# Cross-attention and feed-forward: a fixed TensorE order for the last group of heads, output products one step behind the scores, loads spread over more steps, other PSUM banks for the second pair

## Chip, cores and metric

The kernel runs on one core of one Trainium2 chip. The metric is device time in microseconds (us) for one execution; lower is better. A profile of one execution gives the times of single instructions.

The engines of the core are TensorE (PE, matrix products; the loading of its weights is listed as PEld), VectorE (DVE), ScalarE (ACT), GpSimd (POOL) and SyncE (SP, which here issues nearly all DMAs). Each engine carries out its own list of instructions in a fixed order, and waits in it for semaphores of the others.

## What is computed

One block of cross-attention and a gated feed-forward layer, in float32, on eight batches of 128 tokens of width 512, with 32 heads of width 128. Cut to what matters:

```python
x = x + attention(layernorm(x), ctx, mask, position_bias, ln_weight, w_q, w_k, w_v, w_out)
x = x + ffn(layernorm(x), Wg, Wu, Wd, ag, au, ad)

def attention(h, ctx, m, bias, ...):
    q = heads(rmsnorm(h) * ln_weight @ w_q.T)          # b, 128, 32, 128
    k, v = heads(ctx @ w_k.T), heads(ctx @ w_v.T)
    score = softmax(where(m, einsum('bqhd,bkhd->bhqk', q, k) + bias, -inf))
    attn = einsum('bhqk,bkhd->bqhd', where(m, score, 0), v)
    return h + attn.reshape(b, 128, 32 * 128) @ w_out.T

def ffn(x, ...):
    gate, up = (x @ Wg.T) * ag, (x @ Wu.T) * au        # 1376 wide
    return ((silu(gate) * up) @ Wd.T) * ad
```

## The kernel before

**Groups of heads.** The 32 heads are worked on in eight groups of four (`NG` = 8, `GH` = 4). All queries are projected first (`mm_q`) and stored in HBM as `queries`. Then the loop at line 492 runs over the groups `g`, and inside it line 511 runs over the eight batches `b`. The key and value projections (`mm_k`, `mm_v`) of group g+1 are a Python generator, `products`. It is advanced by three or four product groups per batch (line 520), so that they lie between the attention matmuls of group g.

**Seven products for eight.** Each large product is cut into 2 x 2 blocks and formed from seven block products instead of eight. The sums of blocks that this needs are formed by `sums_a` and `sums_b`: `S_k` and `S_v` of the projection weights on POOL, `T_o` of the output weights on POOL, and `S_a` of the attended values on DVE.

**One batch of attention.** `probabilities` (line 293) adds bias and mask on POOL (L297), forms the scores `sc` on PE (L302), adds the two on DVE, takes the maximum, exponentiates on ACT and divides on DVE. `transpose_p` (line 332) turns the probabilities in 32 x 32 blocks on DVE (`tt`), writes them to HBM (`turned`, L337) and reads them back as `pT` with four DMAs (L342). `attend` (line 354) multiplies by the values (`av`, L358), copies the result out of PSUM on ACT (`aT`) and stores it in HBM as `att`. The variable `pend` keeps three batches between scores and `attend`: scores of batch b are followed by `av` of batch b-3.

**Output products.** `out_products` (line 463) runs over the groups for one pair of batches. For each group `attended` (line 451) loads `a` from `att` (L453) and forms its sums `S_a` (L194 to L197). Then 14 matmuls (28 in the trace's count) go into four PSUM banks `m` (L470). The first pair's output products are interleaved with the last group of heads (line 526), the other three pairs follow after the loop. Each pair is followed by its residual and its second normalization; the transposes of the result (`tp`, L153) stand behind the third output product of the next pair.

**Weights.** `load_wo(g)` loads the output weights of group g, 1 MB, and forms their sums on POOL. The first two are loaded in groups 1 and 2 of the loop. At the start of the last group the pools of the projections are closed (line 503), and in their room a pool `wosB` for five more groups is opened; the eighth group's weights lie in four tiles of the pool `acts`.

**What sets the order.** The program is a list that a scheduler sorts for each engine: an instruction may be placed in front of earlier ones when its operands are expected sooner. Within one engine the resulting order is then fixed. Tiles of a pool wait until the tile before in the same place is released. The lines that set the order in question:

```python
        if g == NG - 1:
            proj.close()
            wos = pools(outp)("wosB", NG - 3, reuse_waits="tile")
...
            advance(3)
            for _ in range(4 if b % 2 else 3):
                next(products, None)
            if g == NG - 1:
                if b < NG - 3:
                    load_wo(b + 2)
                if b < NG - 1:
                    next(first_out)
```

Of the kernel before, what the change touches and what calls it, by code (L numbers as in the profile page):

```python
# [20 lines left out]
MASKED = 3.0e38  # L21
FLOOR = -1.0e38
TINY = 1.0e-30


@with_exitstack
def xattn_ffn_kernel(
# [49 lines left out]
    proj, rows, attn = ExitStack(), ExitStack(), ExitStack()  # L77
    toks = pools(proj)("toks", reuse_waits="tile")
    spool = pools(proj)("spool", 2, reuse_waits="tile")
    wpool = pools(proj)("wpool", 3, reuse_waits="tile")  # L80
    hpool = pools(rows)("hpool", side="right", reuse_waits="tile")
    ps_mm, ps_tp, ps = (pools(attn)(f"ps{n}", 2, space=PSUM) for n in ("mm", "tp", "at"))

    def load_w(name, src):
        t = wpool.tile([P, DC, GW], F32, tag="w", name=name)
# [65 lines left out]
    def transposed(y, tp):  # L151
        for c in range(DC):
            nc.tensor.transpose(tp[:, c, :], y[:, bass.ts(c, P)], ident)  # L153
        return tp
# [138 lines left out]
    def probabilities(g, b, qT, kT, pb):  # L293
        cols = bass.ts(b, S)
        n = f"{g}_{b}"
        s = work.tile([P, GH, S], F32, tag="s", name=f"s_{n}", bufs=3)
        nc.gpsimd.tensor_tensor(  # L297
            s, pb, mneg[:, b : b + 1, :].to_broadcast([P, GH, S]), ALU.add
        )
        sc = ps.tile([P, GH, S], F32, tag="sc", name=f"sc_{n}")  # L300
        for j in range(GH):
            nc.tensor.matmul(  # L302
                sc[:, j, :], qT[:, j, bass.ts(b % 2, S)], kT[j][:, cols], start=True, stop=True
            )
# [49 lines left out]
    def attend(g, b, pT, v):  # L354
        n = f"{g}_{b}"
        av = ps.tile([P, GH, S], F32, tag="av", name=f"av_{n}")
        for j in range(GH):
            nc.tensor.matmul(  # L358
                av[:, j, :], v[b // 2][:, b % 2, bass.ts(j, P)], pT[:, :, j, :],
                start=True, stop=True,  # L360
            )
        aT = work.tile([P, GH, S], F32, tag="aT", name=f"aT_{n}")
        nc.scalar.copy(aT, av)  # L363
        nc.sync.dma_start(att[g][b // 2][:, b % 2], aT)

    pend = []

    def advance(lag):
# [62 lines left out]
    def load_wo(g):  # L431
        src = woT[bass.ts(g, GW), :].rearrange("(c p) n -> p c n", p=P)
        if g == NG - 1:
            up, dn, t12, t4 = (
                acts.tile([P, 2, D], F32, tag="a", name=f"wo{g}_{k}") for k in range(4)
            )
            nc.sync.dma_start(up, src[:, :HC])
            nc.sync.dma_start(dn, src[:, HC:])
            t1, t2, t4 = (
                t.rearrange("p (c n) -> p c n", c=HC) for t in (t12[:, 0], t12[:, 1], t4[:, 0])  # L440
            )
        else:
            w = wos.tile([P, GH, D], F32, tag="w", name=f"wo{g}")
            nc.sync.dma_start(w, src)
            t = wos.tile([P, 3, HC, HW], F32, tag="T", name=f"T_o{g}")
# [17 lines left out]
    def out_products(i, order, banks):  # L463

        m = by_product(banks)
        for g in order:
            sa = attended(g, i)
            for k, n in enumerate((1, 2, 6, 7, 4, 5, 3)):
                for c in range(HC):
                    nc.tensor.matmul(  # L470
                        m[n], sa[n][:, c, :], wo_t[g][n][:, c, :],
                        start=(g == order[0] and c == 0 and k % 2 == 0),
                        stop=(g == order[-1] and c == HC - 1), skip_group_check=True,
                    )
            yield


    def load_bias(g):
# [13 lines left out]
    for g in range(NG):  # L492
        kT, v = kvs.pop(g)
        pb = biases.pop(g)
        if g + 1 < NG:
            biases[g + 1] = load_bias(g + 1)
        if g + 2 < NG:
            kv_w[g + 2] = load_kv(g + 2)
        products = kv(g + 1, kvs) if g + 1 < NG else iter(())
        if g in (1, 2):  # L500
            load_wo(g - 1)
        if g == NG - 1:
            proj.close()
            wos = pools(outp)("wosB", NG - 3, reuse_waits="tile")

            first_banks = [
                pl.tile([P, 2, HW], F32, tag=tag, name=f"m{k}_0")
                for k, (pl, tag) in enumerate(((ps_mm, "mm"), (ps_mm, "mm"), (ps_tp, "pt"), (ps_tp, "pt")))
            ]
            first_out = out_products(0, list(range(NG)), first_banks)  # L510
        for b in range(B):
            if b % 2 == 0:
                qT = ahead.pop((g, b // 2))
                at = todo.index((g, b // 2)) + 2
                if at < len(todo):
                    ahead[todo[at]] = load_queries(*todo[at])
            p = probabilities(g, b, qT, kT, pb)
            pend.append((g, b, transpose_p(g, b, p), v))
            advance(3)
            for _ in range(4 if b % 2 else 3):  # L520
                next(products, None)
# [12 lines left out]
    mv2 = const.tile([P, B, 2], F32, name="mv2")  # L534
    rs2 = const.tile([P, B], F32, name="rs2")

# [36 lines left out]
    def norm2_T(b, y):  # L573
        th, cols = b * S // 512, bass.ds(b * S % 512, S)
        if (0, th) not in h2:
            for f in range(2):
                h2[f, th] = acts.tile([P, HC, 512], F32, tag="a", name=f"h2_{f}_{th}")
        tp = transposed(y, ps.tile([P, DC, P], F32, tag="tp", name="tp2", bufs=1))
        nc.vector.tensor_copy(h2[0, th][:, :, cols], tp[:, :HC])
        nc.scalar.copy(h2[1, th][:, :, cols], tp[:, HC:])  # L580

    x1, ys, banks = [], [], first_banks
    for i in range(B // 2):
        last = i + 1 == B // 2
        order = [2, 3, 4, 5, 6, 7, 0, 1] if last else list(range(NG))
        if i:
            banks = [ps.tile([P, 2, HW], F32, tag="m", name=f"m{k}_{i}") for k in range(4)]
            for n, _ in enumerate(out_products(i, order, banks)):
                if n == 2:
                    for y in ys:  # L590
                        norm2_T(*y)
        m = by_product(banks)
        x1.append(acts.tile([P, 2, D], F32, tag="a", name=f"x1_{i}"))
        for k in range(2):
            b = 2 * i + k
            nc.sync.dma_start(x1[i][:, k, :], x[b])
            nc.scalar.activation(
                x1[i][:, k, :], x1[i][:, k, :], AF.Identity,
                bias=res_bias[:, b : b + 1], scale=res_scale[:, b : b + 1],
            )  # L600
        if last:
            outp.close()
        else:
            residual(i, x1[i], m, banks)
            ys = norm2(i, x1[i])
# [165 lines left out]
```

## Time and profile before

| What | us |
|---|---|
| median of three runs | 1152.23 (1151.07 to 1153.02) |
| profiled execution | 1152.01 |
| its span, first to last instruction | 1150.2 |
| PE busy | 1120.0 (97% of the span) |
| DVE, ACT, POOL busy | 502.3, 318.1, 297.9 |
| output matmuls `m` (L470): mean of one | 0.392 (`wo`,`a` form) |
| scores `sc` and `av`: mean of one | 0.277 |
| POOL bias sum and sums of weights, 128 x 512 | 1.27 |
| `a` from `att`, 512 KB: issue to landing, median | 3.5 |
| `turned`, 256 KB, and `pT`, 64 KB: the same | 2.1 and 2.4 |

Matmuls are pipelined, so the time from one start to the next is shorter than the duration of one: four `m` matmuls that are listed with 1.03 us follow one another every 0.86 us. A wait in brackets in a timeline is idle time of the engine just before the instruction, with what ended it. The page's slices are 28.8 us each.

### The profile page before, as it was taken

How to read it: one execution, taken by the hardware profiler on the slowest of the kernel's cores; microseconds unless marked ns; L12 is line 12 of the kernel's file. 1: busy time of each engine (PE TensorE's matmuls, PEld its weight loads, DVE VectorE, ACT ScalarE, POOL GpSimd, SP SyncE). 2: the span in 40 equal slices, each digit the busy share in tenths (PEclk: the TensorE clock that was granted, in tenths of full speed). 3: DMA queues.
4: the chain of work that ended last, by engine and by line, in shares of the span. 5: the costliest groups of instructions: out<-in, count | busy, mean ns of one | idle time of the engine just before them, and what ended most of it. 6: DMA issues, size and time to landing. Idle time of an engine off the chain costs nothing.

```text
span 1150.2 us, 12321 instructions
## 1 busy us (share of the span) xinstructions
PE 1120.0 (97%) x4286; PEld 731.4 (64%) x4286; DVE 502.3 (44%) x957; ACT 318.1 (28%) x899; POOL 297.9 (26%) x255
## 2 busy tenths in 40 slices
PE   6999999999999999999999999789999999999998
PEld 3564444445867777686958689678888864444445
DVE  4541111116555555555555557824433242434311
ACT  2521112223444344444344443301000022223000
POOL 5331221116333333333223315620000034220000
PEclk9999999999999999999999999899999999999999
DMA  9114432257555455555554347865232332110000
GB/s 284 41 37 149 175 114 110 110 197 259 175 166 175 151 186 174 168 182 183 179 173 152 129 139 218 275 192 171 78 104 65 109 128 73 36 37 1 18 29 28
DMA packets 117533, 154.38 MB, mean 134 GB/s; under 512 B 12032, under 2 KB 71680, under 8 KB 117472
## 3 DMA queue, kind: packets, MB, share of 16 engines
q1 hardware_dynamic: 114784, 149.93, 40.3%
q10 hardware_dynamic: 2192, 2.10, 0.6%
q0 software_dynamic: 496, 1.58, 0.4%
q8 instruction: 34, 0.56, 0.2%
q14 instruction: 27, 0.22, 0.1%
HBM read 101.14 MB, written 52.43 MB: 134 GB/s over the span
## 4 chain that ended last, share of the span: by engine, by line
PE 91%; DVE 4%; DMA 2%; ACT 1%; issue 1%; POOL 0%; SPq 0%; ACTq 0%; DVEq 0%
PE mm_q L262 17%; PE mm_v L280 16%; PE m L470 16%; PE mm_k L262 16%; PE mm_f L690 9%; PE dn L721 7%; PE sc L302 4%; PE av L358 4%; DMA wk<-in_wkT_dram 1%; DMA wo<-in_woT_dram 1%; PE tp L153 1%; PE up L655 1%; PE gp L655 1%; DVE sg L641 1%; ACT s L312 0%
## 5 line engine op out<-in xcount | busy, mean ns | idle before, releaser
L297 POOL TENSOR_TENSOR s<-pb,mneg 128x512 f32<-128x512 f32 x64 | 81.2, 1269 | 291.1 <-DVE tt L335 217.3
L262 PE MATMUL mm_k<-ctx_sb,wk 128*128 128x512 f32 x256 | 117.8, 604 | 7.2 <-DMA wk<-in_wkT_dram 4.4
L280 PE MATMUL mm_v<-wv,ctx_sb 128*128 128x256 f32 x512 | 115.9, 379 | 0.8 <-DMA wv<-in_wvT_dram 0.8
L262 PE MATMUL mm_q<-hT,wq 128*128 128x512 f32 x256 | 112.5, 592 | 0.0
L312 ACT ACTIVATE s<-s,nmx 128x128 f32<-128x128 f32 x256 | 99.5, 390 | 36.0 <-DVE nmx L309 36.0
L470 PE MATMUL m<-wo,a 128*128 128x256 f32 x400 | 101.5, 392 | 6.6 <-DMA a<-att 6.5
L280 PEld LDWEIGHTS mm_v<-wv,ctx_sb 128*128 128x128 f32 x512 | 95.1, 190 | 14.4 <-DMA wv<-in_wvT_dram 1.6
L363 ACT COPY aT<-av 128x512 f32<-128x512 f32 x64 | 37.5, 586 | 203.3 <-PE av L358 105.4
L262 PE MATMUL mm_k<-ctx_sb,S_k 128*128 128x512 f32 x192 | 88.3, 607 | 4.3 <-DVE k L241 3.9
L470 PEld LDWEIGHTS m<-wo,a 128*128 128x128 f32 x400 | 77.7, 197 | 18.0 <-DMA a<-att 6.8
L262 PEld LDWEIGHTS mm_q<-hT,wq 128*128 128x128 f32 x256 | 48.6, 190 | 60.8 <-issue 60.7
L280 PE MATMUL mm_v<-S_v,ctx_sb 128*128 128x256 f32 x384 | 86.6, 381 | 0.0
L262 PEld LDWEIGHTS mm_k<-ctx_sb,wk 128*128 128x128 f32 x256 | 47.2, 194 | 60.1 <-issue 45.5
L262 PE MATMUL mm_q<-hT,S_q 128*128 128x512 f32 x192 | 85.0, 592 | 0.0
L305 DVE TENSOR_TENSOR s<-sc,s 128x512 f32<-128x512 f32 x64 | 44.2, 690 | 86.8 <-PE sc L302 83.6
L280 PEld LDWEIGHTS mm_v<-S_v,ctx_sb 128*128 128x128 f32 x384 | 71.5, 190 | 11.0 <-DVE v L252 1.8
L302 PEld LDWEIGHTS sc<-k,q 128*128 128x128 f32 x512 | 67.3, 194 | 17.4 <-issue 13.4
L721 PE MATMUL dn<-wd,act 128*128 128x512 f32 (+3 forms) x198 | 75.8, 545 | 0.0
L252 DVE TENSOR_TENSOR q<-q,mm_q 128x512 f32<-128x512 f32 x32 | 22.0, 688 | 114.8 <-PE mm_q L262 114.8
L302 PE MATMUL sc<-k,q 128*128 128x128 f32 x512 | 68.1, 277 | 2.0 <-DMA q<-queries 1.9
L358 PE MATMUL av<-pT,v 128*128 128x128 f32 x512 | 68.1, 277 | 0.0
L262 PEld LDWEIGHTS mm_k<-ctx_sb,S_k 128*128 128x128 f32 x192 | 35.4, 192 | 49.3 <-issue 35.7
(156 smaller groups left out, 1492.1 us busy)
## 6 DMA issues: line engine op xcount, KB each, us to landing
queries<-q SPq DMA_DIRECT2D x32, 512.0 KB, 3.8
q<-queries SPq DMA_DIRECT2D x32, 512.0 KB, 4.4
turned<-tt SPq DMA_DIRECT2D x64, 256.0 KB, 2.1
pT<-turned SPq DMA_DIRECT2D x256, 64.0 KB, 2.4
att<-aT SPq DMA_DIRECT2D x64, 256.0 KB, 2.3
a<-att SPq DMA_DIRECT2D x32, 512.0 KB, 3.5
wq<-in_wqT_dram SPq DMA_DIRECT2D x8, 1024.0 KB, 5.5
wk<-in_wkT_dram SPq DMA_DIRECT2D x7, 1024.0 KB, 6.1
```

The lines of the kernel that those rows point to most:

```text
L262: nc.tensor.matmul(out, w[i][:, c, bass.ts(t, P)], src[i][:, c, :], start=(first and c == 0), stop=(c == HC - 1), skip_group_check=True,)
L280: nc.tensor.matmul(out[:, bass.ts(k, HW)], src[i][:, c, bass.ts(2 * t + k, S)], w[i][:, c, :], start=(first and k == 0 and c == 0), stop=( ...
L297: nc.gpsimd.tensor_tensor(s, pb, mneg[:, b : b + 1, :].to_broadcast([P, GH, S]), ALU.add)
L302: nc.tensor.matmul(sc[:, j, :], qT[:, j, bass.ts(b % 2, S)], kT[j][:, cols], start=True, stop=True)
L305: nc.vector.tensor_tensor(s, sc, s, ALU.add)
L312: nc.scalar.activation(s[:, j, :], s[:, j, :], AF.Exp, bias=nmx[:, j : j + 1], accum_out=sm[:, j : j + 1],)
L358: nc.tensor.matmul(av[:, j, :], v[b // 2][:, b % 2, bass.ts(j, P)], pT[:, :, j, :], start=True, stop=True,)
L363: nc.scalar.copy(aT, av)
L470: nc.tensor.matmul(m[n], sa[n][:, c, :], wo_t[g][n][:, c, :], start=(g == order[0] and c == 0 and k % 2 == 0), stop=(g == order[-1] and c ...
L655: nc.tensor.matmul(o[-1][:m], w[:, c, :m], h2[c // HC, th][:, c % HC, :], start=(c == 0), stop=(c == DC - 1),)
L690: nc.tensor.matmul(out, ws[t][n][:, c, :], h2_t[n][:, c, :], start=(first and c == 0), stop=(c == HC - 1), skip_group_check=True,)
L721: nc.tensor.matmul(o, act[ic][:m, bass.ts(b, S)], wd[:m, ic, cols], start=(n == 0), stop=(n == NI - 1),)
```

## The change

Nearly all edits are on the last group of heads and what follows it.

1. In the last group, every PE instruction (scores, `av`, output products) is recorded through `InOrder`, which keeps the order of the program instead of letting the scheduler sort.
2. The first pair's output products begin at batch 1 instead of batch 0, so that product b-1 follows the scores of batch b. Product 7 comes after `av` of batch 5, and before those of batches 6 and 7. `out_products` asks for the attended values of the next group before it forms the products of the present one.
3. In the group before the last, three fewer product groups of the projections are formed; these three follow the first scores of the last group.
4. The pools `spool` (three buffers instead of two) and `wpool` outlive the projections. Output weights 2, 3 and 4 lie in them, loaded as their tiles come free; 2 is asked for in the group before the last. `wosB` has two buffers instead of five. Weights 3 to 6 are asked for at batches 0 to 3 of the last group and weight 7 at batch 5.
5. The pool of the score and `av` banks is opened first, so that the banks of the first pair's products are others than those the second pair then takes; the pool behind them is split in four and three banks, taken in turn (`Turns`).
6. The two transposes of a pair are placed behind the third and the fourth output product of the next pair, instead of both behind the third.

```diff
+class Turns:
+    def __init__(self, *pools):
+        self.pools, self.n = pools, 0
+    def tile(self, *args, **kw):
+        self.n += 1
+        return self.pools[(self.n - 1) % 7 // 4].tile(*args, **kw)
+class InOrder:
...
+            return self.tc.keep_in_program_order(getattr(self.engine, op)(*args, **kw))
...
-    spool = pools(proj)("spool", 2, reuse_waits="tile")
-    wpool = pools(proj)("wpool", 3, reuse_waits="tile")
+    spool = pools(wts)("spool", 3, reuse_waits="tile")
+    wpool = pools(wts)("wpool", 3, reuse_waits="tile")
-    ps_mm, ps_tp, ps = (pools(attn)(f"ps{n}", 2, space=PSUM) for n in ("mm", "tp", "at"))
+    ps, ps_mm, ps_tp = (pools(attn)(f"ps{n}", 2, space=PSUM) for n in ("at", "mm", "tp"))
...
-            w = wos.tile([P, GH, D], F32, tag="w", name=f"wo{g}")
+            held = g in (2, 3, 4)
+            w = (wpool if held else wos).tile([P, GH, D], F32, tag="w", name=f"wo{g}")
...
-        for g in order:
-            sa = attended(g, i)
+        coming = attended(order[0], i)
+        for n, g in enumerate(order):
+            sa = coming
+            if n + 1 < NG and ahead:
+                coming = attended(order[n + 1], i)
...
-        products = kv(g + 1, kvs) if g + 1 < NG else iter(())
+        if g + 1 < NG:
+            products = kv(g + 1, kvs)
...
+        if g == NG - 2:
+            load_wo(2)
         if g == NG - 1:
-            proj.close()
-            wos = pools(outp)("wosB", NG - 3, reuse_waits="tile")
...
-            first_out = out_products(0, list(range(NG)), first_banks)
+            tensor = InOrder(tc, nc.tensor)
...
-            for _ in range(4 if b % 2 else 3):
+            for _ in range(4 if b % 2 and (g < NG - 2 or b == 3) else 3):
                 next(products, None)
             if g == NG - 1:
-                if b < NG - 3:
-                    load_wo(b + 2)
-                if b < NG - 1:
+                if b == 0:
+                    proj.close()
+                    wos = pools(outp)("wosB", 2, reuse_waits="tile")
...
+                    first_out = out_products(0, list(range(NG)), first_banks)
+                if b < NG - 4 or b == 5:
+                    load_wo(b + 3 if b < NG - 4 else NG - 1)
+                if b:
                     next(first_out)
-    load_wo(NG - 1)
+    advance(2)
+    next(first_out)
     advance(0)
-    next(first_out)
+    tensor = nc.tensor
...
-    ps = pool("psO", 7, space=PSUM, reuse_waits="tile")
+    ps = Turns(
+        pool("psA", 4, space=PSUM, reuse_waits="tile"),
+        pool("psB", 3, space=PSUM, reuse_waits="tile"),
+    )
...
-                if n == 2:
-                    for y in ys:
-                        norm2_T(*y)
+            if n in (2, 3):
+                norm2_T(*ys[n - 2])
```

More of the change, by code (lines that the diff above doesn't have):

```diff
@@ L23, with __init__, __getattr__, call @@
 TINY = 1.0e-30
+class Turns:
[5 more added lines that the diff above has]
+class InOrder:
+    def __init__(self, tc, engine):
+        self.tc, self.engine = tc, engine
+    def __getattr__(self, op):
+        def call(*args, **kw):
+            return self.tc.keep_in_program_order(getattr(self.engine, op)(*args, **kw))
+        return call
 @with_exitstack
@@ L75, in xattn_ffn_kernel @@
     small = pool("small", 4, side="right", reuse_waits="tile")
-    proj, rows, attn = ExitStack(), ExitStack(), ExitStack()
+    proj, rows, attn, wts = ExitStack(), ExitStack(), ExitStack(), ExitStack()
+    spool = pools(wts)("spool", 3, reuse_waits="tile")
+    wpool = pools(wts)("wpool", 3, reuse_waits="tile")
     toks = pools(proj)("toks", reuse_waits="tile")
-    spool = pools(proj)("spool", 2, reuse_waits="tile")
-    wpool = pools(proj)("wpool", 3, reuse_waits="tile")
     hpool = pools(rows)("hpool", side="right", reuse_waits="tile")
-    ps_mm, ps_tp, ps = (pools(attn)(f"ps{n}", 2, space=PSUM) for n in ("mm", "tp", "at"))
+    ps, ps_mm, ps_tp = (pools(attn)(f"ps{n}", 2, space=PSUM) for n in ("at", "mm", "tp"))
     def load_w(name, src):
@@ L301, in probabilities @@
         for j in range(GH):
-            nc.tensor.matmul(
+            tensor.matmul(
                 sc[:, j, :], qT[:, j, bass.ts(b % 2, S)], kT[j][:, cols], start=True, stop=True
@@ L357, in attend @@
         for j in range(GH):
-            nc.tensor.matmul(
+            tensor.matmul(
                 av[:, j, :], v[b // 2][:, b % 2, bass.ts(j, P)], pT[:, :, j, :],
@@ L442, in load_wo @@
         else:
-            w = wos.tile([P, GH, D], F32, tag="w", name=f"wo{g}")
+            held = g in (2, 3, 4)
+            w = (wpool if held else wos).tile([P, GH, D], F32, tag="w", name=f"wo{g}")
             nc.sync.dma_start(w, src)
-            t = wos.tile([P, 3, HC, HW], F32, tag="T", name=f"T_o{g}")
+            t = (spool if held else wos).tile(
+                [P, 3, HC, HW], F32, tag="S" if held else "T", name=f"T_o{g}"
+            )
             up, dn, t1, t2, t4 = w[:, :HC], w[:, HC:], t[:, 0], t[:, 1], t[:, 2]
@@ L461, in by_product, with out_products @@
         return {n: banks[k // 2][:, k % 2, :] for k, n in enumerate((1, 2, 6, 7, 4, 5, 3))}
-    def out_products(i, order, banks):
+    def out_products(i, order, banks, ahead=True):
         m = by_product(banks)
-        for g in order:
-            sa = attended(g, i)
+        coming = attended(order[0], i)
[3 more added lines that the diff above has]
+                coming = attended(order[n + 1], i)
             for k, n in enumerate((1, 2, 6, 7, 4, 5, 3)):
                 for c in range(HC):
-                    nc.tensor.matmul(
+                    tensor.matmul(
                         m[n], sa[n][:, c, :], wo_t[g][n][:, c, :],
@@ L475, in out_products @@
             yield
+            if n + 1 < NG and not ahead:
+                coming = attended(order[n + 1], i)
     def load_bias(g):
@@ L498, in xattn_ffn_kernel @@
             kv_w[g + 2] = load_kv(g + 2)
-        products = kv(g + 1, kvs) if g + 1 < NG else iter(())
+        if g + 1 < NG:
+            products = kv(g + 1, kvs)
         if g in (1, 2):
             load_wo(g - 1)
+        if g == NG - 2:
+            load_wo(2)
         if g == NG - 1:
-            proj.close()
-            wos = pools(outp)("wosB", NG - 3, reuse_waits="tile")
[L506 to L509, printed above, removed]
-            first_out = out_products(0, list(range(NG)), first_banks)
+            tensor = InOrder(tc, nc.tensor)
         for b in range(B):
@@ L519, in xattn_ffn_kernel @@
             advance(3)
-            for _ in range(4 if b % 2 else 3):
+            for _ in range(4 if b % 2 and (g < NG - 2 or b == 3) else 3):
                 next(products, None)
             if g == NG - 1:
-                if b < NG - 3:
-                    load_wo(b + 2)
-                if b < NG - 1:
+                if b == 0:
+                    proj.close()
+                    wos = pools(outp)("wosB", 2, reuse_waits="tile")
+                    first_banks = [
+                        pl.tile([P, 2, HW], F32, tag=tag, name=f"m{k}_0")
+                        for k, (pl, tag) in enumerate(2 * [(ps_mm, "mm")] + 2 * [(ps_tp, "pt")])
+                    ]
+                    first_out = out_products(0, list(range(NG)), first_banks)
+                if b < NG - 4 or b == 5:
+                    load_wo(b + 3 if b < NG - 4 else NG - 1)
+                if b:
                     next(first_out)
-    load_wo(NG - 1)
+    advance(2)
+    next(first_out)
     advance(0)
-    next(first_out)
+    tensor = nc.tensor
     attn.close()
-    ps = pool("psO", 7, space=PSUM, reuse_waits="tile")
+    ps = Turns(
+        pool("psA", 4, space=PSUM, reuse_waits="tile"),
+        pool("psB", 3, space=PSUM, reuse_waits="tile"),
+    )
     mv2 = const.tile([P, B, 2], F32, name="mv2")
@@ L577, in norm2_T, with first_residual @@
                 h2[f, th] = acts.tile([P, HC, 512], F32, tag="a", name=f"h2_{f}_{th}")
-        tp = transposed(y, ps.tile([P, DC, P], F32, tag="tp", name="tp2", bufs=1))
+        tp = transposed(y, ps.pools[1].tile([P, DC, P], F32, tag="tp", name="tp2", bufs=1))
         nc.vector.tensor_copy(h2[0, th][:, :, cols], tp[:, :HC])
         nc.scalar.copy(h2[1, th][:, :, cols], tp[:, HC:])
[L582 to L588, printed above, removed]
-                if n == 2:
-                    for y in ys:
-                        norm2_T(*y)
-        m = by_product(banks)
+    x1 = []
+    def first_residual(i):
         x1.append(acts.tile([P, 2, D], F32, tag="a", name=f"x1_{i}"))
@@ L600, in xattn_ffn_kernel @@
             )
+    first_residual(0)
+    residual(0, x1[0], by_product(first_banks), first_banks)
+    ys = norm2(0, x1[0])
+    for i in range(1, B // 2):
+        last = i + 1 == B // 2
+        order = [2, 3, 4, 5, 6, 7, 0, 1] if last else list(range(NG))
+        banks = [ps.tile([P, 2, HW], F32, tag="m", name=f"m{k}_{i}") for k in range(4)]
+        for n, _ in enumerate(out_products(i, order, banks)):
+            if n in (2, 3):
+                norm2_T(*ys[n - 2])
+        m = by_product(banks)
+        first_residual(i)
         if last:
             outp.close()
+            wts.close()
         else:
```

## The prediction

> **What bounds the kernel now.** I began with the page's chain that ended last and its first list, to see which engine sets the end.
>
> ```profile
> PE   6999999999999999999999999789999999999998
> ...
> PE 91%; DVE 4%; DMA 2%; ACT 1%; issue 1%; POOL 0%; SPq 0%; ACTq 0%; DVEq 0%
> ```
>
> TensorE (PE) is busy in every slice except about the 26th, and 91% of the chain is PE. Elsewhere only less PE work would help, and this change leaves the matmuls as they are. So what matters is time in which PE waits or runs slowly. A table of stages prices it (columns: stretch in us; busy us and instructions of PE, PEld, DVE, ACT, POOL; clock; DMA share; GB/s).
>
> ```profile
> 690.00:720.00 30.00, 29.89 (x184) 27.00 (x182) 21.03 (x42) 9.77 (x38) 14.62 (x12) 1.00 0.71 216
> 720.00:775.00 55.00, 44.28 (x212) 38.22 (x212) 30.69 (x54) 12.43 (x48) 25.46 (x19) 0.90 0.73 233
> 775.00:860.00 85.00, 83.63 (x382) 73.05 (x383) 37.84 (x102) 6.85 (x13) 3.94 (x4) 0.97 0.35 116
> 860.00:935.00 75.00, 74.08 (x346) 64.65 (x345) 21.32 (x56) 4.69 (x9) 11.18 (x16) 1.00 0.38 125
> ```
>
> From 720 to 775, PE is idle for 10.7 of 55 us and its clock falls to 0.90. That is the last group of heads. PE's timeline says for whom it waits (start, length, what, and in brackets the wait before it).
>
> ```profile
> 700.49 1.89 PE L470 MATMUL m<-wo,a 128*128 128x256 f32 x8
> ...
> 717.94 1.95 PE L302 MATMUL sc<-k,q 128*128 128x128 f32 x16
> 721.76 1.13 PE L302 MATMUL sc<-k,q 128*128 128x128 f32 x8 [1.87 <-DMA q<-queries]
> ...
> 729.36 3.51 PE L470 MATMUL m<-wo,a 128*128 128x256 f32 x8 [2.80 <-DMA a<-att]
> 735.55 1.12 PE L470 MATMUL m<-T_o,S_a 128*128 128x256 f32 x4 [2.67 <-DVE S_a L195]
> ...
> 749.84 1.05 PE L358 MATMUL av<-pT,v 128*128 128x128 f32 x8
> 750.73 1.89 PE L470 MATMUL m<-wo,a 128*128 128x256 f32 x8
> ...
> 775.45 3.78 PE L470 MATMUL m<-wo,a 128*128 128x256 f32 x8 [3.65 <-DMA a<-att]
> ...
> 803.91 0.66 PE L153 MATMUL tp<-ident,y 128*128 128x128 f32 x4 [0.92 <-ACT h L580]
> ```
>
> Eight output matmuls take 3.51 us at 729.36, after a wait, and 1.89 us at 750.73. A wait is therefore paid twice: once as idle time and once as slow matmuls behind it. At 717.94 the scores of three batches run one after another with nothing between them.
>
> SyncE's (SP) timeline shows why `a` is late at 729: it was issued behind a 1 MB `wo`, and both behind the round trips of the probabilities.
>
> ```profile
> 705.62 0.34 SPq L337 DMA_DIRECT2D turned<-tt  x1
> ...
> 707.83 1.74 SPq L342 DMA_DIRECT2D pT<-turned  x4
> ...
> 714.70 0.34 SPq L337 DMA_DIRECT2D turned<-tt  x1
> ...
> 719.94 0.43 SPq L444 DMA_DIRECT2D wo<-in_woT_dram  x1
> ...
> 722.45 0.43 SPq L453 DMA_DIRECT2D a<-att  x1
> ...
> 754.70 0.43 SPq L453 DMA_DIRECT2D a<-att  x1
> ```
>
> The loss, with batch rows of this timeline: from the scores at 698.71 to the first pair's last product at 784.26 PE has to do 8 scores and 11 `av` of 0.89 us each (start to start, 698.71 to 699.60) and 8 output products of 6.05 us (700.49 to 706.54), 16.9 + 48.4 = 65.3 us. It takes 85.55. **20.2 us are lost**: 11.0 in the four waits in brackets (1.87, 2.80, 2.67, 3.65), the rest at a slow clock.
>
> [...] 3.51 us for eight matmuls against 1.73 (750.73 to 752.46)[...] after waits of 2.80 us already. [...] here `pT` is issued 2.21 us after its `turned` (705.62 to 707.83). [...] an `S_a` sum takes 0.41 us alone and 1.49 us at 741.85 in DVE's timeline, while POOL forms `T_o`. [...] PE shows no wait at 784.26, where the second pair begins, so the trace has nothing to gain there.
>
> **The change, part by part.** *Fixed order.* By the built program, the last group's PE order becomes: scores b, `av` b-3, output product b-1, for each b; then `av`5, product 7, `av`6, `av`7, second pair. One step is 2 x 0.89 + 6.05 = 7.83 us. The run of scores is gone and the 65.3 us of work stay. Nothing can now overtake a late operand: whatever is late stops PE. So I price each product by when its `a` arrives.
>
> *Three value products kept back.* Three stretches of eight `mm_v` matmuls, 5.18 us together (three such stand between two steps in the chain of waits), move from before the last group's first scores to behind them. Cost nil; they cover the first step. Group 6's steps shrink to 6.96 us. Three of them, 20.9 us, must hold scores to `pT`: 6.9 to the issue of `turned` (698.71 to 705.62) + 2.2 + 1.74 for four `pT` + about 2.4 landing = 13.3. Hidden; uncovered it would cost some 1 us a step.
>
> *Weights earlier.* `wo`2, 3, 4 go to the pools of the projection weights, and 2 and 3 are now loaded before the last group begins. Of the chain's 7.50 us DMA and about 5 us POOL around 720 to 733 nothing remains before product 2. POOL does the four sums of `wo`2 in front of the sums for `k`7: eight sums of 1.27 us, 10.2 us, against the 10.4 us from group 6's first scores to the first product that needs them, and the load is issued 6.9 us behind scores that stand two steps, 15.7 us, earlier, so it lands (6.6) 2 us before that count begins. Nil, at worst 2. On SP each moved load is one issue of 0.43 us in steps where SP issues for 2.5 of 7 us: nil. For `wo`5, 6, 7: each stands on SP so that it is issued 22 us or more before its product, against 6.6 us landing and 5.1 us on POOL. Nil on the path, but POOL's sums now lie beside DVE's chain: scores to `turned` took 8.2 us (706.54 to 714.70) with `T_o` beside it, 6.9 without.
>
> *Attended loads.* The order on SP is what the change does not set, and it decides. I count from the start of a batch's scores on PE. Product p is due 0.89 x 4 + 6.05 = 9.6 us after scores p (scores p, `av`, product p-1, scores p+1, `av`).
> Product 2 (scores 2): SP has `turned`2, `att`, then `a`2: 6.9 + 0.35 + 0.40 = 7.7; landed 3.6 later (771.88 to 775.45) at 11.3: a stall of 1.7. Loaded: 8.2, and 6.9 to land (722.45 to 729.36): 6.3. I take 2.5, since `T_o`4 lies beside it and the load of `wo`5 is nearly through.
> Product 3 (scores 3): `a`3 directly behind `turned`3, but also behind `wo`6: 10.9 to 15.5 against 9.6 + 2.5: 0 to 3.4, and its sums beside `T_o`6. I take 2.
> Product 4: `a`4 is behind `pT`3 but two steps ahead: 0.
> Product 5 (scores 5): `a`5 stands behind all four `pT`5: 6.9 + 2.2 + 1.84 = 10.9, landed at 14.5: 4.9. Loaded: 8.2 + 4.4 (755.23 to 759.65) + 1.84 + 6.9 = 21.3: 11.7. I take 6.
> Products 6 and 7: product 5's delay covers them: 0.
> `av`7: DVE takes batch 7's scores only after the sums of `a`7, and then comes a full round trip: 0 to 3.5; 1.
> Slow clock: the wait before product 7 of old cost 8.81 - 6.05 = 2.8 us (775.45 to 784.26). One such for product 5 and 0.7 for the others: 3.5 (2.8 to 7).
> Sum 2.5 + 2 + 6 + 1 + 3.5 = **15.0 us**, against 20.2: a gain of 5.2.
>
> *Other banks, transposes apart.* Banks: nil both ways; the new ones wait for copies of `av` of 0.59 us each, needed 1.7 us later. The two transposes of a pair now stand a product apart: 1.1 us between them (802.83 to 803.91, idle 0.92 in the row) in the second and again in the last pair: 2.2, or nothing if the first is late itself. The weights' pools stay until the last product; the feed-forward weights then wait for a product of the last pair, as they do now, and PE starts on them at 934 without a wait: nil.
>
> Total 7.4. The profiled execution is 1152.01 (span 1150.2 and 1.8 around it), 0.2 below the median of 1152.23, so **1144.6 us**.
>
> **Rivals.** *No stall worth the name:* the loads overtake what I put before them, or arrive sooner. Then all 22.4 go: 1129.6, or 1136 and more where a stall of 6 is left. For it: SP issues are short and DMA is busy only 73%. Against: `pT` must wait for `turned`.
> *Slower:* product 5's `a` behind `pT`5, with a strict PE order. Old PE could put other work there; new PE stands. With the loaded prices (9.7 at product 5, 4 at product 2, 3 at product 3, 2.5 for `av`7, 6 of slow clock) 25.2 are lost, 5.0 more than now, less 2.2 for the transposes: 1154.8; with all at their bounds (11.7, 6.3, 3.4, 3.5, 7: 31.9) 1161.5. It decides from 22.4 us of stall on, some 9 at product 5. I give 1157 as its middle. For it: DMA took 6.9 and 4.4 in this very stretch. Against: `wo`2 to 4 no longer load there.
> *The loss only moves:* stalls of 20.1 to 24.7 us, the same waits behind other names: 1152. For it: each `a` still follows the same round trip. Against: the waits for `wo` and `T_o` have no successor.
>
> **How the numbers follow.** The bound for no change is 0.2% (2.3 us: 1149.7 to 1154.3), about what a measurement tells apart. Forecast (1139 to 1149.7) 0.60, no stall 0.12, moved 0.10, slower 0.18. Faster 0.72, same 0.10, slower 0.18. The range 1136 to 1156 leaves out most of the second case and a third of the last. Since cases of both signs matter: the forecast's own range is 1139.2 (1.7, 0, 4.9, 0 and 2.8: 9.4 lost) to 1149.7.
>
> **What would show it.** Right: in the last group scores and products alternate, no wait for `wo` or `T_o`, waits for `a` before product 5 (some 6 us) and smaller ones before 2 and 3, slow matmuls behind, the second pair's start about 5 us nearer to the last group's first scores, less the moved 5.2 us. No wait at 0.92 us between transposes. Wrong: PE waiting for POOL or `pT`, stalls in group 6, or none before product 5.

## The result, and the profile after

The changed kernel takes 1145.98 us (median of 5 runs, 1144.65 to 1147.76) where the kernel before, run beside it on the same chip, takes 1151.35. The ratio is 0.9954 (95% interval 0.9941 to 0.9967): 5.3 us less, between 3.8 and 6.8. The profiled execution took 1144.65 with a span of 1142.9, so it is the quickest of its five, and 7.3 us of span separate it from the profile of before (1150.2).

TensorE's timeline of the changed kernel in the last group (start, length, what; in brackets the wait before it and what ended it; L45 is the wrapper that records the fixed order):

```profile
694.13 1.05 PE L45 MATMUL sc<-k,q 128*128 128x128 f32 x8
...
710.72 1.89 PE L45 MATMUL m<-wo,a 128*128 128x256 f32 x8
...
721.86 3.55 PE L45 MATMUL m<-wo,a 128*128 128x256 f32 x8 [3.15 <-DMA a<-att]
...
734.81 1.10 PE L45 MATMUL m<-T_o,S_a 128*128 128x256 f32 x4 [1.43 <-DVE S_a L218]
...
747.03 1.05 PE L45 MATMUL sc<-k,q 128*128 128x128 f32 x8
747.92 1.06 PE L45 MATMUL av<-pT,v 128*128 128x128 f32 x8
753.49 3.78 PE L45 MATMUL m<-wo,a 128*128 128x256 f32 x8 [4.51 <-DMA a<-att]
...
762.68 1.05 PE L45 MATMUL sc<-k,q 128*128 128x128 f32 x8
...
779.23 1.89 PE L500 MATMUL m<-wo,a 128*128 128x256 f32 x8
```

Scores and products alternate, and the run of scores of the kernel before is gone. Three waits are left: 3.15 us before product 2 and 4.51 before product 5, both for `a`, and 1.43 in product 3 for the sum `S_a`. Behind the two long ones eight output matmuls take 3.55 and 3.78 us where they take 1.89 elsewhere; the granted clock was 0.54 from 721.86 to 725.50 and 0.50 from 753.49 to 757.30. From the scores at 694.13 to the second pair at 779.23 it is 85.10 us; 65.3 of work and the 5.18 that were moved in make 70.5, so 14.6 us are lost: 9.1 in waits and 5.5 beside them, 4.9 of these in products 2 and 5 (7.8 and 9.2 us instead of 6.05).

The page's slices and its chain have hardly moved (PE 91% of the chain before):

```profile
PE   7899999999999999999999999889999999999998
...
PE 90%; DVE 4%; DMA 3%; ACT 1%; issue 1%; POOL 0%; SPq 0%; ACTq 0%; DVEq 0%; POOLq 0%
```

Apart from the start and the end of the span, two slices of eight tenths are left, at the last group, each 28.6 us long. The table of stages puts numbers to it (columns as before: stretch; busy us and instructions of PE, PEld, DVE, ACT, POOL; clock; DMA share; GB/s):

```profile
690.00:720.00 30.00, 28.71 (x164) 25.93 (x163) 20.97 (x40) 10.27 (x39) 12.05 (x10) 1.00 0.74 231
720.00:780.00 60.00, 52.19 (x260) 45.86 (x261) 35.43 (x76) 13.65 (x50) 17.91 (x15) 0.91 0.63 199
780.00:855.00 75.00, 75.00 (x357) 66.04 (x356) 28.22 (x79) 4.65 (x10) 1.95 (x2) 1.00 0.33 104
```

Before, 10.7 us of idle PE lay between 720 and 775 at a clock of 0.90; now 7.8 of 60 us at 0.91. From 780 to 855 PE is busy throughout; before it was idle for 1.4 of the 85 us from 775 to 860, 0.5 of it the end of the wait for `a` and 0.9 the wait between the transposes.

SyncE's timeline shows where the two `a` stand:

```profile
716.04 0.34 SPq L360 DMA_DIRECT2D turned<-tt  x1
...
716.90 0.46 SPq L480 DMA_DIRECT2D a<-att  x1
...
745.58 0.33 SPq L360 DMA_DIRECT2D turned<-tt  x1
747.63 1.75 SPq L365 DMA_DIRECT2D pT<-turned  x4
749.42 0.44 SPq L480 DMA_DIRECT2D a<-att  x1
```

The `a` of product 2 goes out behind the `turned` of batch 2, and lands 5.0 us later (716.90 to 721.86). The `a` of product 5 goes out behind the four `pT` of batch 5 and lands in 4.1 us (749.42 to 753.49).

The account of the 7.3 us, stage by stage: up to the last group's first scores 694.13 against 698.71, of which 5.18 are the work moved behind them, so 0.6 us worse; the last group 5.6 better (14.6 lost instead of 20.2); from the second pair to the end 363.67 instead of 365.94, 2.3 better.

### The profile page after: what moved, and what is told of

Same layout as the page of the kernel before. It is cut to its first block, busy times and chain, and to the rows that moved or that the text cites. A ratio compares the mean times of both kernels' runs of the same rounds, so it can differ in the third digit from the quotient of the medians.

```text
span 1142.9 us, 12312 instructions
## 1 busy us (share of the span) xinstructions
PE 1116.1 (98%) x4286; PEld 729.4 (64%) x4286; DVE 505.2 (44%) x957; ACT 317.5 (28%) x899; POOL 298.4 (26%) x255
## 4 chain that ended last, share of the span: by engine, by line
PE 90%; DVE 4%; DMA 3%; ACT 1%; issue 1%; POOL 0%; SPq 0%; ACTq 0%; DVEq 0%; POOLq 0%
PE mm_q L285 17%; PE mm_v L303 16%; PE mm_k L285 14%; PE m L500 13%; PE mm_f L739 9%; PE dn L770 7%; PE sc L325 4%; PE m L45 4%; PE av L381 4%; DMA a<-att 1%; DMA wv<-in_wvT_dram 1%; ACT s L335 1%; PE av L45 1%; PE tp L176 1%; PE gp L704 1%
## 5 line engine op out<-in xcount | busy, mean ns | idle before, releaser
L500 PE MATMUL m<-wo,a 128*128 128x256 f32 x300 | 72.6, 379 | 0.0
L325 PEld LDWEIGHTS sc<-k,q 128*128 128x128 f32 x448 | 58.7, 192 | 14.8 <-issue 13.4
L285 PEld LDWEIGHTS mm_q<-hT,S_q 128*128 128x128 f32 x192 | 36.5, 190 | 45.9 <-issue 45.9
L770 PEld LDWEIGHTS dn<-wd,act 128*128 128x128 f32 (+1 forms) x198 | 37.6, 190 | 38.5 <-issue 37.4
L500 PEld LDWEIGHTS m<-wo,a 128*128 128x128 f32 x300 | 56.5, 190 | 7.4
```

The costliest lines, as they stand in the source:

```text
L285: nc.tensor.matmul(out, w[i][:, c, bass.ts(t, P)], src[i][:, c, :], start=(first and c == 0), stop=(c == HC - 1), skip_group_check=True,)
L325: tensor.matmul(sc[:, j, :], qT[:, j, bass.ts(b % 2, S)], kT[j][:, cols], start=True, stop=True)
L500: tensor.matmul(m[n], sa[n][:, c, :], wo_t[g][n][:, c, :], start=(g == order[0] and c == 0 and k % 2 == 0), stop=(g == order[-1] and c == ...
L770: nc.tensor.matmul(o, act[ic][:m, bass.ts(b, S)], wd[:m, ic, cols], start=(n == 0), stop=(n == NI - 1),)
```

## The experiments

All edits are to the changed kernel. Each run has its own runs of the kernel before beside it, so the ratios are the fair comparison; 0.001 is 1.15 us. "Lost" is the time from the last group's first scores to the second pair beyond 70.5 us of work (65.3 where nothing was moved), "rest" the time from there to the end of the span, both from the profile. A profiled execution can lie up to 2.4 us from the median of its kernel, so these two columns say where the time goes, and the ratio says how much it is.

| Kernel | median us | ratio to before (95%) | lost | rest |
|---|---|---|---|---|
| before | 1151.35 | 1 | 20.2 | 365.9 |
| changed | 1145.98 | 0.9954 (0.9941 to 0.9967) | 14.6 | 363.7 |
| free order | 1140.30 | 0.9899 (0.9883 to 0.9915) | 8.7 | 363.7 |
| weights as before | 1152.20 | 0.9998 (0.9988 to 1.0008) | 22.9 | 363.6 |
| both | 1145.70 | 0.9953 (0.9938 to 0.9967) | 16.8 | 363.7 |
| `a` asked for early | 1136.66 | 0.9870 (0.9855 to 0.9884) | 3.0 | 364.8 |
| the same, free order | 1134.87 | 0.9855 (0.9838 to 0.9872) | 3.1 | 364.6 |
| early `a`, free order, weight 6 later | 1138.28 | 0.9885 (0.9865 to 0.9904) | 6.7 | 364.5 |
| `a` early, weights as before | 1144.34 | 0.9936 (0.9919 to 0.9953) | 15.9 | 363.6 |
| transposes together | 1147.41 | 0.9958 (0.9943 to 0.9973) | 15.3 | 363.7 |
| no request ahead, pairs 2 to 4 | 1150.29 | 0.9991 (0.9983 to 1.0000) | 14.2 | 367.9 |
| banks as before | 1145.21 | 0.9952 (0.9939 to 0.9966) | 13.1 | 363.6 |
| no products kept back | 1149.06 | 0.9972 (0.9962 to 0.9983) | see text | 363.7 |

**The place of the `a` loads.**

```diff
                 coming = attended(order[n + 1], i)
+            if not i:
+                yield
...
+            if g == NG - 1 and b:
+                next(first_out)
             p = probabilities(g, b, qT, kT, pb)
```

> The changed kernel with one edit: in the last group the next `a` is asked for at the head of a batch, ahead of its `probabilities`, so that on SyncE the loads for products 2 and 3 stand a whole step earlier than the `turned` they followed, and the load for product 5 stands before `pT`4. Theory (what is left of the loss is the place of the `a` loads on SyncE): the waits before products 2, 3 and 5 (3.15, 1.43, 4.51 us) go and so does most of the 5.5 us of slow matmuls behind them; at most 3 us are left, so 1132 to 1136 us. Rival (the core's queues[...] are simply full at this place): waits of the same sum come back for `S_a`, `T_o` or `pT`, 1142 to 1149 us.

SyncE and TensorE of this kernel:

```profile
711.33 0.34 SPq L360 DMA_DIRECT2D turned<-tt  x1
711.76 0.38 SPq L480 DMA_DIRECT2D a<-att  x1
```

```profile
718.67 1.05 PE L45 MATMUL sc<-k,q 128*128 128x128 f32 x8
...
720.46 1.89 PE L45 MATMUL m<-wo,a 128*128 128x256 f32 x8
...
739.85 1.10 PE L45 MATMUL m<-T_o,S_a 128*128 128x256 f32 x4 [1.84 <-DVE S_a L218]
```

The `a` of product 2 now goes out at 711.76, 6.9 us before the scores of batch 3 (718.67), where it went out 0.14 us behind them (716.90 and 716.76). Product 2 starts without a wait, and so does product 5. One wait of 1.84 us and one of 0.30 are left, at product 4 for sums of its `a` on DVE. The lost time falls from 14.6 to 3.0 us, and the ratio by 0.0084, 9.7 us; the median of 1136.66 lies 0.7 above the range of the theory and far below the rival's. What the change still loses is thus set mainly by the place of `a` on SyncE, not by full queues: the waits go while the DMA engines are busier than in the changed kernel (a share of 0.77 from 690 to 720 us and 0.68 from 720 to 770, against 0.74 and 0.64). (The rest is 1.1 us longer; PE waits for DVE for 0.51 us at 771.64, in the second pair's first product.)

**The fixed order and the early weights.** Two edits, alone and together:

```diff
-            tensor = InOrder(tc, nc.tensor)
+            tensor = nc.tensor
```

> The changed kernel without the fixed order: the scheduler sorts the last group's TensorE work again. In its order scores 3, 4, 5 and 6, 7 bunch and products 6 and 7 come together at the end. Theory (what counts is when each `a` arrives, a strict order lets the whole step stand): the bunched scores fill some of the 9.1 us of waits but products 3 to 7 then wait for their `a`, which stand behind more `turned` on SyncE: idle 8 to 14 us in the last group, 1147 to 1153 us. Rival (a free order covers the waits): idle below 5 us, 1139 to 1144 us.

```diff
-    spool = pools(wts)("spool", 3, reuse_waits="tile")
-    wpool = pools(wts)("wpool", 3, reuse_waits="tile")
+    spool = pools(proj)("spool", 2, reuse_waits="tile")
+    wpool = pools(proj)("wpool", 3, reuse_waits="tile")
...
-            held = g in (2, 3, 4)
+            held = False
...
-        if g == NG - 2:
-            load_wo(2)
...
-                    wos = pools(outp)("wosB", 2, reuse_waits="tile")
+                    wos = pools(outp)("wosB", NG - 3, reuse_waits="tile")
...
-                if b < NG - 4 or b == 5:
-                    load_wo(b + 3 if b < NG - 4 else NG - 1)
+                if b < NG - 3 or b == 5:
+                    load_wo(b + 2)
```

> The changed kernel with the output weights handled as before: all projection pools close at the start of the last group, `wosB` has five buffers, weights 2 to 6 are loaded at batches 0 to 4, `spool` has two buffers; order, lag and transposes stay. Theory A (the earlier weights are the source of the gain): waits for `wo` or `T_o` return before products 2 to 5, and 1150 to 1156 us. Theory B (the lag of one step gives even the late weights time: issued near 702, 7 us landing, 5 us of sums on POOL, due at 718): no wait for `wo` or `T_o` of over 0.5 us; only the `a` loads land slower beside 5 MB of weights, 1145 to 1149 us.

And both edits together:

> The changed kernel with the output weights handled as before and without the fixed order: the lag of one step, the kept products and the transposes stay. With the three kernels already measured it makes a table of two by two (order fixed or free, weights early or as before). Theory (both parts act on one thing, the place of the `a` loads, and add up): the free order saves the 5.7 us that it saved with early weights, so 1145 to 1148 us. Rival (with late weights the scheduler runs through the scores of five batches and then stands before the products, as in the kernel before): 1149 to 1153 us, with waits of 8 to 12 us in the last group.

The theory on the free order fell and its rival held by its time; the waits of the last group come to 5.8 us (0.98, 0.39, 0.29, 1.81, 2.33), a little over the 5 that the rival allowed. TensorE in free order:

```profile
718.30 1.05 PE L325 MATMUL sc<-k,q 128*128 128x128 f32 x8
...
720.08 1.06 PE L325 MATMUL sc<-k,q 128*128 128x128 f32 x8
...
721.87 0.83 PE L325 MATMUL sc<-k,q 128*128 128x128 f32 x6
723.68 2.00 PE L500 MATMUL m<-wo,a 128*128 128x256 f32 x8 [0.98 <-DMA a<-att]
```

While `a` is on its way, the scores of batch 4, an `av` and most of the scores of batch 5 fill the place in which the fixed order stands still; product 2 comes with a wait of 0.98 us instead of 3.15. The table of two by two: the fixed order costs 6.3 us with early weights (0.9954 to 0.9899) and 5.2 with late ones (0.9998 to 0.9953); the early weights bring 5.1 in fixed and 6.2 in free order. The two add up by their times (with late weights in free order one long wait of 10.55 us for `S_a` stands behind waits of 1.38 and 1.05, so the rival's picture came with the theory's time), and in the change they cancel: the kernel with neither is as fast as the change (0.9953 and 0.9954). By the time lost in the profiles they add up too, but don't quite cancel: the order costs 5.9 and 6.1 us, the early weights bring 8.3 and 8.1 (the profile of the kernel with weights as before lies 1.7 us above its median).

```profile
738.92 2.04 PE L500 MATMUL m<-T_o,S_a 128*128 128x256 f32 x4 [10.55 <-DVE S_a L218]
```

The change's net gain is what these two edits don't touch: 3.4 us less lost in the last group (20.2 to 16.8), and 2.2 us in what follows it. The step between scores and products, the request ahead in the first pair and the kept products can each have a part in the 3.4; only the kept products were taken back alone (below), so how it divides stays open.

With late weights the time is that of theory A, but the waits are those of theory B: no wait names `wo` or `T_o`.

```profile
717.80 1.05 PE L45 MATMUL sc<-k,q 128*128 128x128 f32 x8
...
728.79 3.75 PE L45 MATMUL m<-wo,a 128*128 128x256 f32 x8 [9.04 <-DMA a<-att]
```

```profile
718.19 0.46 SPq L469 DMA_DIRECT2D wo<-in_woT_dram  x1
719.47 1.74 SPq L365 DMA_DIRECT2D pT<-turned  x4
721.26 0.43 SPq L480 DMA_DIRECT2D a<-att  x1
```

`a` is late again. A 1 MB `wo` and the `pT` of batch 2 stand in front of it, so it goes out 3.5 us behind the scores of batch 3 (717.80), not 0.14, and lands in 7.5 us instead of 5.0: 3.3 + 2.6 = 5.9 us, and the wait is longer by as much (9.04 against 3.15). So at this product the early weights pay because `wo` is out of the way of `a`. A further run was to show whether that is all:

> The changed kernel with the output weights handled as before, the fixed order kept, and the `a` of the next product asked for at the head of the batch. Theory (the early weights are worth their 6.2 us only because they clear SyncE and the DMA ahead of `a`): with `a` asked for early the late weights cost at most 2 us against the same kernel with early weights (1136.7), so 1136 to 1139 us, and no wait names `wo` or `T_o`. Rival (the weights are needed early for themselves): waits for `wo`, `T_o` or POOL before products 2 to 4, 1141 to 1147 us.

It shows that it is not. With `a` asked for early and the weights as before, 0.9936 is 7.6 us above 0.9870, far over the 2 allowed. The time lies in the rival's range, yet its waits for `wo` or `T_o` don't come either. The waits in products 2 to 4 (1.71, 0.48, 1.69 us) are for `S_a`; the long one is at product 6:

```profile
762.58 3.75 PE L45 MATMUL m<-wo,a 128*128 128x256 f32 x8 [6.42 <-DMA a<-att]
```

```profile
757.29 0.37 SPq L365 DMA_DIRECT2D pT<-turned  x1
757.71 0.44 SPq L480 DMA_DIRECT2D a<-att  x1
```

Its `a` goes out in the middle of the `pT` of batch 6. The waits stay waits for attended values, at another product. POOL may have a part in them, as the rival has it: POOL forms sums of weights from 716.69 to 722.19 us, across the wait of product 2 (719.50 to 721.21), and takes 1.52 and 1.45 us for the last two of four, against 1.27 for each of the first two. How long DVE took for its sums there was not shown. Which of SyncE's queue, the DMA load and the sums on POOL does most of this wasn't separated.

**Free order and early `a` together.**

> The changed kernel with the `a` of the next product asked for at the head of the batch and without the fixed order. Theory (the fixed order costs only what its waits cost, and with early `a` some 2.1 us of waits, 1.84 and 0.30, are left): within 2 us of the same kernel in fixed order, 1134.5 to 1137.5 us. Rival (the order itself is worth some 5.7 us whatever the loads do): 1130 to 1132 us.

1134.87 us, as the theory has it: with `a` in time the order is worth nothing that the intervals can tell (0.9870, 0.9855). This is the best version found; it beats the kernel before by 16 to 17 us and the change by some 11. One more step was tried from here, with weight 6, that of the seventh group, asked for at batch 4 instead of 3, so that the `a` of product 4 moves forward:

```diff
-                if b < NG - 4 or b == 5:
-                    load_wo(b + 3 if b < NG - 4 else NG - 1)
+                if b < 3 or b in (4, 5):
+                    load_wo(b + 3 if b < 3 else b + 2)
```

> The changed kernel in free order, `a` asked for at the head of the batch, and the output weights of the seventh group asked for one batch later, so that the `a` of product 4 stands directly behind `turned`3 on SyncE. Theory (what is left is the 1.67 us wait for the sums of that `a`): it goes, no more than 1 us of waits stays in the last group, 1131.5 to 1134 us. Rival (POOL then forms the later weights' sums beside DVE's sums of the next `a`, and a wait of the same size moves to product 5 or 6): 1134.5 to 1137 us.

The wait at product 4 is gone, and one of 3.68 us stands before product 6 (6.7 us lost instead of 3.1; the ratio is 3.5 us worse, with intervals that just overlap):

```profile
756.74 3.78 PE L502 MATMUL m<-wo,a 128*128 128x256 f32 x8 [3.68 <-DMA a<-att]
```

```profile
753.05 0.32 SPq L365 DMA_DIRECT2D pT<-turned  x1
753.42 0.42 SPq L480 DMA_DIRECT2D a<-att  x1
```

The time lies above both ranges. The rival was right about the place, and not about the cause: product 6 waits for its `a`, which again goes out behind the first `pT` of batch 6, not for sums beside POOL.

**Behind the second pair's start: transposes, banks, request ahead.**

```diff
-            if n in (2, 3):
-                norm2_T(*ys[n - 2])
+            if n == 2:
+                for y in ys:
+                    norm2_T(*y)
```

> The changed kernel with both transposes of a pair behind the third product again. Theory: a wait of about 0.9 us before the second transpose returns in at least two of the three pairs, 1.1 us each: 2.2 us more than the changed kernel, 1147.5 to 1149 us. Rival (the 2.3 us gained behind the second pair's start come from the other PSUM banks or from elsewhere): no such waits, 1145 to 1147 us.

```profile
799.98 0.60 PE L176 MATMUL tp<-ident,y 128*128 128x128 f32 x4
800.42 1.46 PE L500 MATMUL m<-wo,a 128*128 128x256 f32 x6
801.72 0.60 PE L176 MATMUL tp<-ident,y 128*128 128x128 f32 x4
```

The scheduler puts six recorded matmuls (three of the program) between the two transposes by itself. No wait, and 363.7 us to the end as in the changed kernel: the theory fell. The banks (the old pool order and one pool of seven) are not it either:

> The changed kernel with the PSUM pools opened in the order of before and one pool of seven banks behind them. Theory: nothing, since TensorE did not wait at the start of the second pair in the kernel before: 1145 to 1147 us, second pair's start to the end of the span 363 to 364 us. Rival (the 2.3 us gained behind that start come from the banks): 1147.5 to 1149 us, some 366 us.

363.6 us to the end, ratio 0.9952. What was left is that pairs two to four now ask for `a` one group ahead. Two runs take that back and leave the transposes split. In the first, pairs two to four use the attended values of the fifth group of their order for all products but the first, with as many and as large loads; the second uses each group's own (its inner loop has a variable of its own, as this branch reads `n` behind it).

```diff
-        for n, _ in enumerate(out_products(i, order, banks)):
+        for n, _ in enumerate(out_products(i, order, banks, ahead=False)):
```

> The changed kernel, but pairs two to four ask for the attended values of a group only when its products are formed, as before; the two transposes stay split in the program. In the built order they stand side by side again in the second and the last pair. Theory (it is the early request, not the split, that holds the transposes apart, since the scheduler moves a transpose ahead of a product whose `a` it expects late): a wait of 0.9 us before the second transpose in two pairs, 365.5 to 366.5 us behind the second pair's start, 1147.5 to 1149 us. Rival (the split decides): no such wait, 1145 to 1147 us.

> The changed kernel, but pairs two to four ask for the attended values of a group only after the products of the group before, as the old kernel did, and each group's own values; the transposes stay split. Theory (the early request holds the transposes apart): two waits of 0.9 us before the second transpose and 1 to 2 us more from later loads, 365.5 to 367.5 us behind the second pair's start against 363.7, 1147.5 to 1150 us. Rival (the split decides): 363.7 us, 1145 to 1147 us.

```profile
798.33 0.60 PE L176 MATMUL tp<-ident,y 128*128 128x128 f32 x4
799.85 0.66 PE L176 MATMUL tp<-ident,y 128*128 128x128 f32 x4 [0.92 <-ACT h L623]
...
901.76 1.96 PE L704 MATMUL gp<-h,wg 128*96 128x512 f32 x4 [1.67 <-DMA wg<-in_wgT_dram]
```

The transposes stand side by side again, although the program splits them, and both waits of 0.92 us are back, exactly as in the kernel before. A wait of 1.67 for `wg`, which the kernel before does not have, comes with them. It is 367.9 us to the end, 4.2 more, and the ratio gives 4.3 (0.9991); the two waits between transposes make 2.2 of that, at 1.1 each, and the wait for `wg` most of the rest. The first of the two runs reads the same (1150.79 us, ratio 0.9998, 367.5 to the end). So the request ahead holds the transposes apart. That the scheduler then expects the product's operand sooner, and so no longer puts the second transpose in front of it, is the likely reason; only the order and the waits are shown.

**Products kept back.**

```diff
-            for _ in range(4 if b % 2 and (g < NG - 2 or b == 3) else 3):
+            for _ in range(4 if b % 2 else 3):
```

> The changed kernel without the three value products kept back: 5.18 us of work stand again before the last group's first scores. Theory (the kept products cover the round trip of the first batch): the two waits of 0.67 us in the group before go, but the last group starts with 1.8 us of work where it had 7, the round trip to product 2 is as long as before, and the wait before products 1 and 2 grows by 3 to 5 us with slow matmuls behind it: 1148 to 1152 us. Rival (three batches between scores and `av` are cover enough): 1144.5 to 1146.5 us.

```profile
718.74 1.05 PE L45 MATMUL sc<-k,q 128*128 128x128 f32 x8
...
731.18 3.53 PE L45 MATMUL m<-wo,a 128*128 128x256 f32 x8 [10.50 <-DMA a<-att]
...
758.71 1.99 PE L45 MATMUL m<-wo,a 128*128 128x256 f32 x8 [2.24 <-DMA a<-att]
```

The wait moves where the theory says, and further: 10.50 us before product 2 where it was 3.15, while that before product 5 shrinks from 4.51 to 2.24; the two waits in the group before are gone. But in the profile it comes to nothing: from the seventh group's first scores to the second pair it takes 143.9 us here (637.53 to 781.41) and 143.8 in the changed kernel (635.40 to 779.23), since only one of the two waits now leaves slow matmuls behind it (3.53 and 1.99 us for eight). The medians say 2.1 us worse (22 runs), with intervals that overlap by 0.0005; this profile lies 2.2 us below its median, that of the change 1.3. Between nothing and 2 us; not settled.

## Why the prediction was right, and where it was not

The sum came out: 1144.6 predicted and 1144.65 profiled, 7.4 us of gain predicted and 7.3 found. That it came out to a tenth is luck. The waits were priced at 11.5 us and came to 9.1, the slow matmuls at 3.5 and came to 5.5, and 0.6 us ahead of the last group were priced at nil; these errors nearly cancel. What was right is that late `a` loads decide, and which products wait. Its parts, in its own order:

- *Fixed order.* "Nothing can now overtake a late operand" was right, and so was pricing each product by its `a`. The step that is missing is a price for the order itself. It costs 5.2 to 6.3 us; with early weights the trace of the free order shows bunched scores in the place of these waits. The prediction noted that the run of scores is gone, and didn't ask what it had covered.
- *Kept products.* Priced at nil in both groups. Two waits of 0.43 and 0.24 us came up in the seventh group, as its shorter steps wait for PSUM to be copied out:

```profile
641.22 1.98 PE L285 MATMUL mm_k<-ctx_sb,wk 128*128 128x512 f32 x4 [0.43 <-ACT k L259]
655.60 1.98 PE L285 MATMUL mm_k<-ctx_sb,wk 128*128 128x512 f32 x4 [0.24 <-ACT k L269]
```

- *Weights earlier.* `wo` and `T_o` have indeed left the chain of waits. But with the order fixed late weights don't bring them back once the products run a step later, so that reason was the old kernel's. The early weights bring 5.1 to 6.2 us, for which the prediction has no term of its own; the largest part that the traces show is the `a` that they no longer delay.
- *Attended loads.* 15.0 us lost were predicted, 14.6 found. Product 2: 2.5 against 3.15. Product 3: 2 against 1.43; it waits for a sum of `a`, not for `a` itself. The sums began at 732.84, behind DVE's work on the scores of batch 4, and the second took 1.37 us, where the median of its 32 is 0.42, beside a sum of `T_o` on POOL (1.51 us from 732.87, against 1.26 to 1.27 for the three before it; DVE's timeline):

```profile
732.84 0.41 DVE L217 TENSOR_TENSOR S_a<-a 128x256 f32<-128x256 f32 x1
733.29 1.37 DVE L218 TENSOR_TENSOR S_a<-S_a,a 128x256 f32<-128x256 f32 x1
```

  Product 5: 6 against 4.51. Its `a` went out 10.2 us behind the scores and landed in 4.1, close to the lower of the two prices (10.9 and 3.6, a stall of 4.9) between which the 6 was taken. `av`7: 1 against 0. Products 4, 6 and 7: 0, right.
- *Slow clock.* 3.5 against 5.5. The prediction counted one wait with a full stretch of slow matmuls behind it; there were two, of 3.15 and 4.51 us. Product 2 took 7.8 us instead of 6.05, product 5 took 9.2.
- *Transposes.* 2.2 against 2.3, the right size for the wrong edit. The split alone does nothing; the request one group ahead, to which the prediction gave no price for the later pairs, removes the two waits.
- *Banks.* Nil, as predicted and as the run shows.
- *Against the median.* The gain is 5.3 us by the medians and 7.3 between the two profiles; the prediction was made against one profile, which lay 0.2 us from its median, while the new one lies 1.3 below its own. The lower end of the prediction's own range, 1139.2, is counted from that median and its other times from the profile, 0.2 apart.

Of the rivals, "no stall" described what came only with another edit: `a` asked for early, in free order, took 1134.87. "The loss only moves" was right in kind, as each wait left is again for `a` or its sums, but wrong in size: 14.6 us, not 20.1 and more. "Slower" needed some 9 us at product 5, where 4.51 came.

## What to carry to other kernels

When an order is fixed, ask what the scheduler's own order was filling. A run of early work that looks untidy in the trace may be what covers a late load. While `a` was late the fixed order cost 5.2 to 6.3 us; once it was early the order made no difference that the runs can tell, so no run here shows a fixed order to pay. First put the loads that the bottleneck engine waits for ahead of round trips in the same DMA queue: the requests for `a`, moved forward by one step, were worth 9.7 us here, more than the whole change. And a request moved earlier can change the order of instructions on another engine far from it, as it did for the transposes; take an edit back alone before it gets the credit.

## What the runs showed of the hardware

In these runs no one length of wait parts the slow matmuls from the fast. Waits of 2.24 us (the kernel without kept products, shown above) and 2.27 (banks as before) left eight `m` matmuls at 1.99 us. A wait of 2.33 in free order was followed by slow matmuls, and so was one of 2.20 in the second run without the request ahead:

```profile
753.26 2.05 PE L381 MATMUL av<-pT,v 128*128 128x128 f32 x8 [2.33 <-DMA pT<-turned]
755.10 2.61 PE L500 MATMUL m<-wo,a 128*128 128x256 f32 x8
```

```profile
722.27 3.48 PE L45 MATMUL m<-wo,a 128*128 128x256 f32 x8 [2.20 <-DMA a<-att]
```

In the first, eight `av` take 2.05 us, not 1.05, and the first eight `m` behind them 2.61, not 1.89; in the second, eight `m` take 3.48. Slow matmuls also came a little after the wait. In the kernel before, the four behind the wait of 2.67 us took 1.12 us, but each of the next two fours took 1.89, not 1.03, at a granted clock of 0.50 (736.49 to 739.88):

```profile
736.49 1.89 PE L470 MATMUL m<-wo,a 128*128 128x256 f32 x4
```

With early `a` and weights as before it happened after two short waits, 1.71 and 0.30 us:

```profile
721.21 1.10 PE L45 MATMUL m<-T_o,S_a 128*128 128x256 f32 x4 [1.71 <-DVE S_a L218]
722.62 2.05 PE L45 MATMUL m<-wo,a 128*128 128x256 f32 x4 [0.30 <-DVE a L219]
```

The same pair of waits, 1.84 and 0.30 us, left no slow matmuls with early `a` and early weights (1.10 us behind each). So of the four waits between 2.20 and 2.33 us two were followed by 0.1 us more for the matmuls behind them, and two by 1.6 to 1.7 us more; what decides between these cases wasn't found.
